# A two-layer model on one Trainium2 core: FP4 down products in three parts a block, gate and up interleaved over six PSUM banks

## The chip, the cores and the metric

The kernel runs on one core of a Trainium2 chip. The engines of that core work side by side, each from a queue of its own: TensorE (PE, with its weight loads shown apart as PEld), VectorE (DVE), ScalarE (ACT), GpSimd (POOL), and SyncE (SP), which here only issues DMAs. Matrix products land in PSUM, eight banks of 128 x 512 fp32 words, and DVE or ACT has to read a bank out before TensorE may write it again. The metric is the device time of one execution in microseconds (us).

## The reference

The input x is 2 x 1024 tokens of width 512. Four layers follow one another, each as `x = layernorm(x + layer(x))`: a linear attention, a feed-forward layer with FP4 weights, a gated linear attention in chunks of 64, and a feed-forward layer that takes the 512 best-scored tokens of a sequence. The change touches the second one alone:

```python
w_gu   = dequant_fp4(gate_up_packed, gate_up_scales)   # [2816, 512], a scale for each 128 inputs
w_down = dequant_fp4(down_packed, down_scales)         # [512, 1408]
gate_up = x @ w_gu.T
gate, up = gate_up[..., :1408], gate_up[..., 1408:]
h = silu(gate) * up
y = h @ w_down.T
y = y / sqrt(mean(y*y, axis=-1) + 1e-6)
x = layernorm(x + y)
```

All arithmetic is fp32. The gate and up products take x in two fp32r parts (x1Th, the rounded value, and x1Tl, the rest), so that two quick matmuls stand for one fp32 matmul.

## The kernel before

**Tiling.** The tokens are cut into NB = 4 blocks of 512. In the FP4 layer a block has NI = 11 passes, f = 0 to 10, one for each 128 of the 1408 hidden units. A pass makes a gate tile and an up tile, 128 units x 512 tokens each. Each is a sum over KC = 4 groups of 128 inputs, and because every group has a scale of its own the groups can't be summed in PSUM: each group (two matmuls, the x1Th one and the x1Tl one, L458) gets a bank, and the bank is then added with its scale to a tile in SBUF. Group k = 0 is written by ACT (L463, called g0 and u0 below); groups 1 to 3 are added by DVE (L468, g1 to g3 and u1 to u3). Where a pass is called `alone` or `by_three`, u3 goes to ACT (L465) and POOL (L466) instead. ACT then applies silu to the gate tile (L634), and POOL multiplies the two into a chunk of h (L635). The gate and up tiles have two rooms each, taken in turn by f.

**The down product.** y of a block is computed from h and wdn one block later, in seven-product form (Strassen's): P1 to P7 and a small P8 for the odd eleventh chunk. The function `down` is a generator that yields before each of its 78 steps; a step is one fp32 matmul of 256 columns (L501 or L510), which the trace shows as two entries. `take(pieces, n)` runs it on by n yields. POOL makes the sums that the products need (`sums`, L516), and DVE adds the products to y (L525 to L544).

**Staging.** Before the change the steps of the last block's products are spread over the passes: five yields ahead of pass 0, then eight or nine behind each of the passes 0 to 8, and none behind passes 9 and 10. During passes 9 and 10 the x of the next block is turned: eight PE transposes (L190) behind each of the two passes, then ACT copies (L204) and DVE differences (L205) that make x1Th and x1Tl. The block before that, whose y is complete, is normed in `old_steps`: ACT squares (L577), POOL takes the inverse root (`power`, L581 and L582), ACT scales y (L586), POOL adds y to x (L591), DVE takes statistics (L181, L182), POOL norms x (L560). After the four blocks a tail of seven `take` calls runs the last block's products, together with the transposes and logits of the next layer.

**Order.** A planner (Tile's scheduler) sets the order in each engine's queue. Code that comes earlier has the right of way among what it believes ready; `tc.issue_after(ins)` puts what is traced in it behind `ins` on that engine. So `issue_after(mm)` holds the order on PE, `issue_after(sl)` that on ACT behind the silu, `issue_after(hm)` that on POOL behind the product h. Engines take their queues in order.

**Banks.** Two pools of four banks: `mm_bank` serves gate, up and the transposes, `acc_bank` the products P1 to P8. In `alone` passes the groups with odd k use the second pool too, so that eight banks take turns.

Of the kernel before, what the change touches and what calls it, by code (L numbers as in the profile page):

```python
# [10 lines left out]
F32 = mybir.dt.float32  # L11
# [10 lines left out]
P = 128  # L22
B, T, C = 2, 1024, 512
NB = 4
# [49 lines left out]
def body(ctx: ExitStack, tc: tile.TileContext, a: dict, out: bass.AP):  # L74
# [7 lines left out]
    pmm = ctx.enter_context(tc.tile_pool(name="pmm", bufs=4, space=PSUM))  # L82
    pacc = ctx.enter_context(tc.tile_pool(name="pacc", bufs=4, space=PSUM))
    dram = ctx.enter_context(tc.tile_pool(name="dram", bufs=1, space=DRAM))

    def mm_bank(name):
        return pmm.tile([P, 512], F32, tag="mm", name=name)

    def acc_bank(name):
        return pacc.tile([P, 512], F32, tag="acc", name=name)  # L90
# [343 lines left out]
    with tc.tile_pool(name="s2", bufs=1) as wk2:  # L434
# [17 lines left out]
        def scaled_sum(f, parts, name, by_three, eight_banks):  # L452

            acc = rooms[name][f % 2]
            for k in range(KC):
                ps = (acc_bank if eight_banks and k % 2 else mm_bank)(f"{name}p")
                for x in parts:
                    ins = nc.tensor.matmul(  # L458
                        ps, wgu[:, k, f * P : (f + 1) * P], x[:, k], start=x is parts[0], stop=x is parts[1]
                    ).ins  # L460
                s = scale[:, k * FG + f : k * FG + f + 1]
                if k == 0:
                    nc.scalar.activation(acc, ps, AF.Copy, scale=s)  # L463
                elif k == KC - 1 and by_three:
                    nc.scalar.activation(spare, ps, AF.Copy, scale=s)  # L465
                    nc.gpsimd.tensor_add(acc, acc, spare)  # L466
                else:
                    last = nc.vector.scalar_tensor_tensor(acc, ps, s, acc, ALU.mult, ALU.add).ins  # L468
            return acc, ins, last
# [18 lines left out]
        of_S = lambda j: S[:, j]  # L488

        def down(h, y_of):  # L490

            A11, A12, A21, A22 = (h.block(e, s) for s in range(2) for e in range(2))

            def whole(name, x, w, tail=None):

                ps = acc_bank(name)
                for r in range(2):
                    cut = ps[:, 256 * r : 256 * r + 256]
                    for j in range(NP):
                        yield  # L500
                        nc.tensor.matmul(  # L501
                            cut, x(j)[:, r], w[:, j], start=j == 0, stop=j == NP - 1 and tail is None
                        )
                    if tail is not None:
                        yield
                        of_last(cut, r, *tail, start=False)
                return ps.rearrange("p (r c) -> p r c", r=2)

            def of_last(cut, r, s, o, start):
                nc.tensor.matmul(  # L510
                    cut, h.last(s)[:, r], wdn[:, NI - 1, 256 * o : 256 * o + 256], start=start, stop=True
                )

            def sums(op, dst, x, y):
                for j in range(NP):
                    ins = nc.gpsimd.tensor_tensor(dst(j), x(j), y(j), op).ins  # L516
                return ins

            sums(ALU.add, of_S, A21, A22)
            p1 = yield from whole("P1", A11, B11)  # L520
            p2 = yield from whole("P2", A12, B21, (0, 0))
            p5 = yield from whole("P5", of_S, T1)
            c11, c12, c21, c22 = y_of()
            nc.scalar.copy(c21, p1)
# [12 lines left out]
            nc.vector.tensor_add(c22, c12, p7)  # L537
            p8 = acc_bank("P8")
            for r in range(2):
                yield  # L540
                of_last(p8[:, 256 * r : 256 * r + 256], r, 1, 1, start=True)
# [20 lines left out]
        class Normed:  # L562
# [57 lines left out]

        wsums = sums_of_wdn()
        now, pieces = None, iter(())
        for blk in range(NB):
            h = Hidden(blk)
            for f in range(NI):
                if f == 0:
                    if blk:
                        with tc.issue_after(mm), tc.issue_after(hm):
                            take(pieces, 5)

                alone = blk == 0 or f >= NI - 2
                gate, mm, st = scaled_sum(f, parts, "gate", False, alone)
                up, mm, st = scaled_sum(NI + f, parts, "up", alone, alone)
                sl = nc.scalar.activation(gate, gate, AF.Silu).ins  # L634
# [762 lines left out]
```

## Time and profile before

| what | value |
|---|---|
| median of 3 runs | 1033.77 us (1033.0 to 1033.81) |
| the profiled execution's own time | 1033.33 us |
| its span, first to last instruction | 1031.6 us |
| TensorE busy in the span | 999.9 us (97%) |
| mean granted TensorE clock | 0.995 |
| stretch of the FP4 layer's four blocks | 254.3 to 554.3 us |
| its tail, to the next layer | to about 604 us |

The page gives the busy time of each engine and groups of like instructions; the timeline gives single instructions with their start, length and, in brackets, the idle time of the engine ahead of them with the instruction that ended it. A matmul of 512 columns is shown some 0.40 us long, but such matmuls overlap: what one costs is the distance from its start to the next start. All of what follows is read in that way.

### The profile page before, as it was taken

To read this page: it belongs to the slowest core of one execution; us is meant where nothing else is said; L and a number is where in the kernel's file an instruction comes from. 1 tells how busy PE (TensorE), PEld (TensorE's weight loads), DVE (VectorE), ACT (ScalarE), POOL (GpSimd) and SP (SyncE) were. 2 spreads that over 40 slices of the span, in tenths; PEclk is the share of its full clock that TensorE was granted. 3 is DMA by queue.
4 is the path that set the end of the run, shared out by engine and by line. 5 is a ranking of instruction groups with operands and counts; after the bars stand their busy time and mean duration, and the time that the engine had idled before them with its cause. 6 is when DMAs were issued, how large, how long until landed. Compare 5 with 4: busy or idle time off the path is not lost.

```text
span 1031.6 us, 10932 instructions
## 1 busy us (share of the span) xinstructions
PE 999.9 (97%) x4061; PEld 706.7 (69%) x4061; DVE 651.5 (63%) x1225; ACT 283.9 (28%) x469; POOL 306.1 (30%) x281
## 2 busy tenths in 40 slices
PE   8999999999999998999999999999999999999996
PEld 3454444545767776777778955687687688888885
DVE  1246745376875675675677139446788886689744
ACT  2223232222652244234324043242121123221000
POOL 1100351003785634554556403101005003000022
PEclk9999999999999999999999999999999999999999
DMA  9611123100000000000002050000002422140011
GB/s 346 194 46 56 42 69 98 31 31 0 1 1 1 1 1 0 1 1 1 1 0 93 1 213 1 1 1 1 1 1 82 124 81 82 41 141 24 1 41 41
DMA packets 25688, 48.81 MB, mean 47 GB/s; under 512 B 4652, under 2 KB 6316, under 8 KB 25123
## 3 DMA queue, kind: packets, MB, share of 16 engines
q1 hardware_dynamic: 22995, 42.85, 12.5%
q0 software_dynamic: 1920, 4.22, 1.1%
q10 hardware_dynamic: 720, 1.05, 0.3%
q8 instruction: 32, 0.52, 0.2%
q14 instruction: 21, 0.17, 0.1%
HBM read 39.70 MB, written 10.52 MB: 49 GB/s over the span
## 4 chain that ended last, share of the span: by engine, by line
PE 71%; DVE 10%; issue 9%; ACT 5%; POOL 4%; DMA 0%; POOLq 0%; DVEq 0%; ACTq 0%
PE P L501 11%; PE yp L1141 9%; PE hp L1062 7%; PE qp L210 5%; PE xk L279 5%; PE upp L458 5%; PE ao L210 5%; PE kp L210 4%; DVE gate L468 3%; PE gatep L458 3%; PE ao L945 3%; PE go L901 2%; ACT gate L463 2%; PE kp L296 1%; PE lp L425 1%
## 5 line engine op out<-in xcount | busy, mean ns | idle before, releaser
L468 DVE SCALAR_TENSOR_TENSOR gate<-gatep,scale,gate 128x512 f32<-128x512 f32 x132 | 98.6, 749 | 76.2 <-ACT gate L463 69.8
L174 POOL TENSOR_TENSOR rs<-rs,table 128x4 f32<-128x4 f32 (+1 forms) x21 | 19.6, 936 | 321.2 <-DVE rs L173 320.7
L468 DVE SCALAR_TENSOR_TENSOR up<-upp,scale,up 128x512 f32<-128x512 f32 x115 | 85.9, 747 | 8.1 <-ACT up L463 1.5
L458 PE MATMUL upp<-x1Th,wgu 128*128 128x512 f32 x176 | 75.8, 432 | 10.6 <-ACT gate L463 7.9
L458 PE MATMUL gatep<-x1Th,wgu 128*128 128x512 f32 x176 | 74.5, 430 | 1.2 <-ACT x1Th L204 1.1
L458 PE MATMUL upp<-x1Tl,wgu 128*128 128x512 f32 x176 | 70.5, 403 | 0.0
L458 PE MATMUL gatep<-x1Tl,wgu 128*128 128x512 f32 x176 | 68.6, 399 | 0.1
L635 POOL TENSOR_TENSOR h<-up,gate 128x512 f32<-128x512 f32 x32 | 40.8, 1276 | 87.8 <-DVE up L468 79.7
L501 PE MATMUL P<-wdn,h 128*128 128x256 f32 x256 | 61.9, 379 | 0.0
L458 PEld LDWEIGHTS upp<-x1Th,wgu 128*128 128x128 f32 x176 | 33.6, 191 | 38.2 <-DVE gate L468 18.2
L463 ACT ACTIVATE gate<-gatep,scale 128x512 f32<-128x512 f32 x44 | 30.3, 688 | 104.3 <-PE gatep L458 89.7
L210 PE MATMUL ao<-G,qT 128*128 128x512 f32 x128 | 57.6, 595 | 0.0
L210 PE MATMUL qp<-Wq,x0T 128*128 128x512 f32 x128 | 57.6, 592 | 0.0
L279 PE MATMUL xk<-k,x 128*128 128x512 f32 x128 | 56.7, 592 | 0.0
L945 PE MATMUL ao<-W1o,uT 128*128 128x512 f32 x128 | 55.6, 592 | 0.0
L501 PEld LDWEIGHTS P<-wdn,h 128*128 128x128 f32 x256 | 48.2, 190 | 6.7
L849 POOL TENSOR_TENSOR sum<-sum,sq 128x512 f32<-128x512 f32 x12 | 19.0, 1582 | 107.8 <-issue 84.5
L264 DVE SCALAR_TENSOR_TENSOR k<-kp,e 128x512 f32<-128x512 f32 x16 | 11.0, 691 | 55.4 <-ACT e L263 49.4
L279 PEld LDWEIGHTS xk<-k,x 128*128 128x128 f32 x128 | 24.3, 190 | 30.6 <-issue 29.9
L210 PEld LDWEIGHTS ao<-G,qT 128*128 128x128 f32 x128 | 24.0, 190 | 30.0 <-issue 28.7
L945 PEld LDWEIGHTS ao<-W1o,uT 128*128 128x128 f32 x128 | 24.0, 190 | 28.7 <-issue 28.0
L210 PE MATMUL kp<-Wk,x0T 128*128 128x512 f32 x96 | 43.3, 593 | 0.2 <-DVE k L264 0.2
(335 smaller groups left out, 2131.0 us busy)
## 6 DMA issues: line engine op xcount, KB each, us to landing
pk<-in_gu SPq DMA_DIRECT2D x16, 352.0 KB, 3.8
x<-in_x SPq DMA_DIRECT2D x4, 1024.0 KB, 12.8
w<-in_w SPq DMA_DIRECT2D x1, 4096.0 KB, 14.5
xs<-picked SPq DMA_DIRECT2D x4, 1024.0 KB, 5.0
out<-x SPq DMA_DIRECT2D x4, 1024.0 KB, 4.3
w<-in_w SPq DMA_DIRECT2D x4, 1024.0 KB, 6.4
x0T<-in_xT SPq DMA_DIRECT2D x3, 1024.0 KB, 8.8
pk<-in_dn SPq DMA_DIRECT2D x11, 256.0 KB, 3.5
```

What stands on the lines that cost most here:

```text
L174: power = nc.gpsimd.tensor_tensor(rs[:, :n], rs[:, :n], const("mhalf")[:, :n], ALU.pow).ins
L210: nc.tensor.matmul(ps, lhs[:, k], w[:, k], start=start and k == 0, stop=stop and k == KC - 1)
L279: nc.tensor.matmul(acc[c], x_t[2 * b + i // 4][:, i % 4, c * P : (c + 1) * P], k, start=i == 0, stop=i == 7)
L458: ins = nc.tensor.matmul(ps, wgu[:, k, f * P : (f + 1) * P], x[:, k], start=x is parts[0], stop=x is parts[1]).ins
L463: nc.scalar.activation(acc, ps, AF.Copy, scale=s)
L468: last = nc.vector.scalar_tensor_tensor(acc, ps, s, acc, ALU.mult, ALU.add).ins
L501: nc.tensor.matmul(cut, x(j)[:, r], w[:, j], start=j == 0, stop=j == NP - 1 and tail is None)
L635: hm = nc.gpsimd.tensor_mul(h.chunk(f), up, gate).ins
L901: nc.tensor.matmul(ps[:, 256 * m : 256 * m + 256], w[:, k, m], b[:, k, 256 * half : 256 * half + 256], start=k == 0, stop=k == KC - 1,)
L945: nc.tensor.matmul(ao[i], uT[blk][:, k, i * P : (i + 1) * P], W1o[:, k], start=n == 0, stop=n == 3)
L1062: nc.tensor.matmul(ps[:, 256 * j : 256 * j + 256], w[:, k, 2 * g + j], x[:, k], start=k == 0, stop=k == 1)
L1141: nc.tensor.matmul(ps[:, 256 * r : 256 * r + 256], x(r, j), w(j), start=j == 0, stop=j == NJ - 1)
```

## The change

It does five things, all in the FP4 layer.

1. The steps of the down product are no longer spread. Pass 0 starts the generator with one yield (the POOL sums alone, no matmul); 22 steps (P1, P2) run behind pass 2, 32 (P5, P4, P6) behind pass 5 and 24 (P7, P8, P3) behind pass 8.
2. Each product is added to y as soon as it ends, where before the adding of P1 and P2 waited for the end of P5, and that of P4 and P5 for the end of P6. For that, y's room is asked for after P1, not after P5.
3. Gate and up take turns group by group (`scaled_sums`): g0, u0, g1, u1, and so on, each pass behind the last matmul of what went before. Gate, up and transposes get six banks (0 to 3, 6, 7), the products two (4, 5); `alone` is gone, and u3 goes to ACT and POOL in block 0 and in passes 9 and 10, as before. In the tail the banks are four and four again.
4. The rooms of the gate and up tiles alternate over the whole layer, so that pass 0 no longer takes the room that pass 10 has just used.
5. Of the old block's norm, the inverse root moves from step 1 to step 0, statistics and the first two tiles' norm to step 2. In block 3 the squares and the root of block 2 are traced behind pass 9, and the rest of that norm ahead of the tail.

```diff
-    pmm = ctx.enter_context(tc.tile_pool(name="pmm", bufs=4, space=PSUM))
-    pacc = ctx.enter_context(tc.tile_pool(name="pacc", bufs=4, space=PSUM))
+    psum = ctx.enter_context(tc.tile_pool(name="psum", bufs=1, space=PSUM))
+    rings, turn_of = {"mm": range(4), "acc": range(4, 8)}, {"mm": 0, "acc": 0}
+    def bank(ring, name):
+        i = rings[ring][turn_of[ring] % len(rings[ring])]
+        turn_of[ring] += 1
+        return psum.tile([P, 512], F32, tag=f"bank{i}", name=name)
...
-        def scaled_sum(f, parts, name, by_three, eight_banks):
-
-            acc = rooms[name][f % 2]
+        def scaled_sums(f, parts, gate, up, by_three):
+
             for k in range(KC):
...
+                for acc, at, name in ((gate, f, "gatep"), (up, NI + f, "upp")):
+                    ps = mm_bank(name)
+                    for x in parts:
+                        ins = nc.tensor.matmul(
+                            ps, wgu[:, k, at * P : (at + 1) * P], x[:, k], start=x is parts[0], stop=x is parts[1]
+                        ).ins
+                    s = scale[:, k * FG + at : k * FG + at + 1]
+                    if k == 0:
+                        nc.scalar.activation(acc, ps, AF.Copy, scale=s)
+                    elif k == KC - 1 and acc is up and by_three:
+                        nc.scalar.activation(spare, ps, AF.Copy, scale=s)
+                        nc.gpsimd.tensor_add(acc, acc, spare)
+                    else:
+                        last = nc.vector.scalar_tensor_tensor(acc, ps, s, acc, ALU.mult, ALU.add).ins
+            return ins, last
...
             p1 = yield from whole("P1", A11, B11)
-            p2 = yield from whole("P2", A12, B21, (0, 0))
-            p5 = yield from whole("P5", of_S, T1)
             c11, c12, c21, c22 = y_of()
             nc.scalar.copy(c21, p1)
+            p2 = yield from whole("P2", A12, B21, (0, 0))
             nc.vector.tensor_add(c11, c21, p2)
+            p5 = yield from whole("P5", of_S, T1)
+            nc.vector.tensor_add(c12, c21, p5)
             ins = sums(ALU.subtract, of_S, of_S, A11)
+            with tc.issue_after(ins):
+                ins = sums(ALU.subtract, A21, A11, A21)
+            with tc.issue_after(ins):
+                sums(ALU.subtract, A12, A12, of_S)
             p4 = yield from whole("P4", A22, T4, (1, 0))
-            with tc.issue_after(ins):
-                sums(ALU.subtract, A21, A11, A21)
+            nc.vector.tensor_add(c21, c21, p4)
             p6 = yield from whole("P6", of_S, T2)
-            nc.vector.tensor_add(c12, c21, p6)
-            nc.vector.tensor_add(c21, c12, p4)
-            nc.vector.tensor_add(c12, c12, p5)
-            sums(ALU.subtract, A12, A12, of_S)
+            nc.vector.tensor_add(c12, c12, p6)
+            nc.vector.tensor_add(c21, c21, p6)
             p7 = yield from whole("P7", A21, B12)
+            nc.vector.tensor_add(c22, c12, p7)
             nc.vector.tensor_add(c21, c21, p7)
-            nc.vector.tensor_add(c22, c12, p7)
             p8 = acc_bank("P8")
...
                 return {
-                    0: lambda: self.squares(range(4)),
-                    1: lambda: (self.power(), self.scaled(), self.to_x((0, 1))),
-                    2: lambda: self.to_x((2, 3)),
-                    4: self.stats,
-                    5: lambda: self.norm((0,)),
-                    7: lambda: self.norm((1,)),
+                    0: lambda: (self.squares(range(4)), self.power()),
+                    1: lambda: (self.scaled(), self.to_x((0, 1))),
+                    2: lambda: (self.to_x((2, 3)), self.stats(), self.norm((0, 1))),
                     8: lambda: self.norm((2, 3)),
                 }
...
+        rings["mm"], rings["acc"] = (0, 1, 2, 3, 6, 7), (4, 5)
...
-                if f == 0:
-                    if blk:
-                        with tc.issue_after(mm), tc.issue_after(hm):
-                            take(pieces, 5)
-
-                alone = blk == 0 or f >= NI - 2
-                gate, mm, st = scaled_sum(f, parts, "gate", False, alone)
-                up, mm, st = scaled_sum(NI + f, parts, "up", alone, alone)
+                if f == 0 and blk:
+                    with tc.issue_after(hm):
+                        take(pieces, 1)
+                gate, up = (rooms[n][(blk * NI + f) % 2] for n in ("gate", "up"))
+                with tc.issue_after(mm) if blk or f else ExitStack():
+                    mm, st = scaled_sums(f, parts, gate, up, blk == 0 or f >= NI - 2)
                 sl = nc.scalar.activation(gate, gate, AF.Silu).ins
                 hm = nc.gpsimd.tensor_mul(h.chunk(f), up, gate).ins
                 with tc.issue_after(mm), tc.issue_after(st), tc.issue_after(hm), tc.issue_after(sl):
-                    if f < NI - 2:
-                        take(pieces, 9 if f in (0, NI - 3) else 8)
                     if blk == 0 and f in (2, 4, 6, 8):
                         norm_tiles(3, late, (f // 2 - 1,))
-                    for _ in range((2, 2, 2, 0, 1, 1)[f] if blk == 1 and f < 6 else 0):
+                    for _ in range((1, 1, 4, 1, 1)[f] if blk == 1 and f < 5 else 0):
                         next(wsums)
                     if blk > 1 and f in old_steps:
                         old_steps[f]()
+
+                    if blk and f in (2, 5, 8):
+                        take(pieces, {2: 22, 5: 32, 8: 24}[f])
+                        mm = last_p[0]
...
+                        if blk == NB - 1 and f == NI - 2:
+                            now.squares(range(4))
+                            now.power()
...
+        rings["mm"], rings["acc"] = range(4), range(4, 8)
+        with tc.issue_after(st):
+            for _ in old.rest():
+                pass
         for n, steps in enumerate((11, 12, 10, 12, 10, 10, 14)):
             with tc.issue_after(mm), tc.issue_after(hm):
                 take(pieces, steps)
-            if n == 0:
-                old.squares(range(4))
-                old.power()
-            if n == 1:
-                for _ in old.rest():
-                    pass
```

More of the change, by code (lines that the diff above doesn't have):

```diff
@@ L81, in body @@
     sp = ctx.enter_context(tc.tile_pool(name="small", bufs=3))
-    pmm = ctx.enter_context(tc.tile_pool(name="pmm", bufs=4, space=PSUM))
-    pacc = ctx.enter_context(tc.tile_pool(name="pacc", bufs=4, space=PSUM))
+    psum = ctx.enter_context(tc.tile_pool(name="psum", bufs=1, space=PSUM))
     dram = ctx.enter_context(tc.tile_pool(name="dram", bufs=1, space=DRAM))
+    rings, turn_of = {"mm": range(4), "acc": range(4, 8)}, {"mm": 0, "acc": 0}
[3 more added lines that the diff above has]
+        return psum.tile([P, 512], F32, tag=f"bank{i}", name=name)
     def mm_bank(name):
-        return pmm.tile([P, 512], F32, tag="mm", name=name)
+        return bank("mm", name)
     def acc_bank(name):
-        return pacc.tile([P, 512], F32, tag="acc", name=name)
+        return bank("acc", name)
     table = cpool.tile([P, _TABLE.shape[1]], F32, name="table")
@@ L450, in sums_of_wdn @@
                     yield nc.gpsimd.tensor_sub(dst[:, j], x[:, j], y[:, j])
-        def scaled_sum(f, parts, name, by_three, eight_banks):
-            acc = rooms[name][f % 2]
+        def scaled_sums(f, parts, gate, up, by_three):
             for k in range(KC):
[L456 to L469, printed above, removed]
+                for acc, at, name in ((gate, f, "gatep"), (up, NI + f, "upp")):
[13 more added lines that the diff above has]
+            return ins, last
         class Hidden:
@@ L488, in body @@
         of_S = lambda j: S[:, j]
+        last_p = [None]
         def down(h, y_of):
@@ L500, in whole @@
                         yield
-                        nc.tensor.matmul(
+                        last_p[0] = nc.tensor.matmul(
                             cut, x(j)[:, r], w[:, j], start=j == 0, stop=j == NP - 1 and tail is None
-                        )
+                        ).ins
                     if tail is not None:
                         yield
-                        of_last(cut, r, *tail, start=False)
+                        last_p[0] = of_last(cut, r, *tail, start=False)
                 return ps.rearrange("p (r c) -> p r c", r=2)
             def of_last(cut, r, s, o, start):
-                nc.tensor.matmul(
+                return nc.tensor.matmul(
                     cut, h.last(s)[:, r], wdn[:, NI - 1, 256 * o : 256 * o + 256], start=start, stop=True
-                )
+                ).ins
             def sums(op, dst, x, y):
@@ L540, in down @@
                 yield
-                of_last(p8[:, 256 * r : 256 * r + 256], r, 1, 1, start=True)
+                last_p[0] = of_last(p8[:, 256 * r : 256 * r + 256], r, 1, 1, start=True)
             nc.vector.tensor_add(c22, c22, p8.rearrange("p (r c) -> p r c", r=2))
```

## The prediction, made before the changed kernel was run

> **What bounds the kernel now.** I read the page first, then the four blocks as stretches, then one pass on PE, DVE and ACT.
>
> Page, parts 1 and 2:
>
> ```profile
> span 1031.6 us, 10932 instructions
> ...
> PE 999.9 (97%) x4061; PEld 706.7 (69%) x4061; DVE 651.5 (63%) x1225; ACT 283.9 (28%) x469; POOL 306.1 (30%) x281
> ...
> PE   8999999999999998999999999999999999999996
> ```
>
> PE is the bound nearly everywhere, so the change can win only where PE waits between 254 and 604 us. How much that is must come from starts, not from busy time. Blocks 1, 2 and 3 in the view of stretches (length, then busy time of PE, PEld, DVE, ACT, POOL, granted clock):
>
> ```profile
> 301.70:384.40 82.70, 80.26 (x349) 62.67 (x349) 54.56 (x77) 25.76 (x40) 43.53 (x42) 1.00 0.00 0
> 384.40:470.70 86.30, 81.73 (x348) 63.62 (x348) 56.86 (x86) 30.98 (x52) 45.80 (x45) 0.98 0.00 1
> 470.70:554.30 83.60, 79.90 (x340) 62.19 (x341) 54.39 (x82) 31.47 (x57) 45.88 (x46) 0.98 0.04 13
> ```
>
> The same matmuls back to back, by their spacing in the PE timeline: a gate or up matmul 0.234 us, so a pass of 16 takes 3.74; a down step 2 x 0.216 = 0.432; eight transposes 0.87. A whole block is 11 x 3.74 + 78 x 0.432 + 2 x 0.87 = 76.6 us (74.9 in block 3's stretch, which has four steps less). So 6.1, 9.7 and 8.7 us are waits. One ordinary pass, on PE:
>
> ```profile
> 357.05 0.58 PE L458 MATMUL gatep<-x1Th,wgu 128*128 128x512 f32 x1
> ...
> 359.84 0.40 PE L458 MATMUL upp<-x1Tl,wgu 128*128 128x512 f32 x1
> 360.36 0.50 PE L458 MATMUL upp<-x1Th,wgu 128*128 128x512 f32 x1
> ...
> 364.66 0.59 PE L458 MATMUL gatep<-x1Th,wgu 128*128 128x512 f32 x1
> ```
>
> From pass to pass 7.61 us, against 3.74 + 8 x 0.432 = 7.20. The loss sits at 359.84 to 360.36: u2 needs a bank that DVE hasn't read. DVE itself:
>
> ```profile
> 358.70 2.46 DVE L468 SCALAR_TENSOR_TENSOR gate<-gatep,scale,gate 128x512 f32<-128x512 f32 x3 [0.75 <-ACT gate L463]
> 361.08 2.45 DVE L468 SCALAR_TENSOR_TENSOR up<-upp,scale,up 128x512 f32<-128x512 f32 x3
> ...
> 408.22 0.74 DVE L468 SCALAR_TENSOR_TENSOR gate<-gatep,scale,gate 128x512 f32<-128x512 f32 x1
> 408.88 1.60 DVE L468 SCALAR_TENSOR_TENSOR up<-upp,scale,up 128x512 f32<-128x512 f32 x2
> ```
>
> Three additions to one tile take 2.46, 0.82 each; where a gate follows on an up (408.22 to 408.88) the distance is 0.66. Next, the large wait of block 2, pass 2 (block 3 has its twin at 491.9), from the timelines of ACT and PE and the stretch behind:
>
> ```profile
> 402.36 2.56 ACT L586 ACTIVATE y<-y,ms 128x512 f32<-128x512 f32 x4 [4.53 <-POOL ms L582]
> 404.82 0.67 ACT L463 ACTIVATE gate<-gatep,scale 128x512 f32<-128x512 f32 x1
> 405.54 0.50 PE L458 MATMUL upp<-x1Th,wgu 128*128 128x512 f32 x1 [2.67 <-ACT gate L463]
> 406.00:410.00 4.00, 3.94 (x11) 2.77 (x10) 3.37 (x6) 1.32 (x2) 0.00 (x0) 0.57 0.00 0
> ```
>
> The scaling of y stands ahead of g0 in ACT's queue and waits for POOL's root; PE idles 2.67 us and then runs at a granted clock of 0.57. Last, the border between blocks (PE, then ACT):
>
> ```profile
> 381.06 1.03 PE L190 MATMUL x1Tp<-table,x 128*128 128x128 f32 x8
> 381.93 1.89 PE L501 MATMUL P<-wdn,h 128*128 128x256 f32 x8
> 384.37 0.97 PE L458 MATMUL gatep<-x1Th,wgu 128*128 128x512 f32 x3 [0.55 <-ACT x1Th L204]
> ...
> 382.73 0.63 ACT L634 ACTIVATE gate<-gate 128x512 f32<-128x512 f32 x1 [0.72 <-DVE gate L468]
> 383.27 1.05 ACT L204 CAST x1Th<-x1Tp 128x512 fp32r<-128x512 f32 x2
> ```
>
> The next block can't start before the casts, which stand behind the silu of pass 10; four down steps (1.73 us) fill that hole today.
>
> **The waits, summed.** From starts of passes: (A) passes 1 to 8 without the two large waits lose 9.2 us (22 passes, 0.34 to 0.75 each). (B) The two passes 2, 12.02 and 11.76 us long instead of 7.20, lose 9.4. (C) Passes 0 last 9.69, 8.75 and 8.78 instead of 7.63, 4.3. (D) The borders, start of pass 9 to next pass 0: 11.66 and 11.65 against 10.97; with the first one like them, 2.1. (E) Block 0 waits about 2.1 (ACT's g0 waits for POOL's h). Together 27.1 us: the most that can be won.
>
> **Interleaving and six banks.** DVE's six additions cost 6 x 0.66 = 3.96 a pass in place of 4.9, ACT's g0 and u0 run beside. Passes 0 to 2, 3 to 5 and 6 to 8 now follow without products between. In such a run DVE starts 1.86 us behind PE and falls back 0.22 a pass. Six banks let PE lead by 6 x 0.47 = 2.8 us; followed bank by bank, the first to be late is u2 of the third pass, by 0.1. Nine runs, 0.9 us. The products then give DVE 9.5, 13.8 or 10.4 us to catch up, so (A) is gone but for that. In block 0 POOL has 7.24 us per two passes (four at 1.29, one norm tile at 2.08) against PE's 7.49; I leave 0.4 of (E).
>
> **Two banks for products.** P3 takes P7's bank while P8 (0.86 us) is all that lies between. Two additions at 0.66 and the 0.28 from matmul to DVE make some 1.65, so PE waits 0.8. Three blocks, 2.4. The others have four us or more between end and reuse: nothing; if DVE were late there, each would cost up to 0.7. y's room comes free only when POOL has added y to x behind pass 2; P1's copy then waits, but its bank is next used by P5, behind pass 5: nothing. POOL's sums for P6 (5 x 0.71 = 3.6 us from the end of P5) end 1.4 us before P6.
>
> **Norm steps.** The four squares take 3.0 us of ACT (0.75 each), the scaling 2.56, and no product lies there any more to cover them. ACT's own work is 3 x 0.58 = 1.7 a pass, so in three passes (11.2 us) there is room; what counts is the order. g0 of the next pass is there 0.92 us after that pass starts, u0 at 1.39, the silu only when DVE has ended g3, about 1.6: g0 and u0 should precede the silu and all behind it. Then g0 of pass 2 comes about 1 us late, inside the banks' lead: 0.5 in blocks 2 and 3, 1.0 in place of (B). The root behind POOL's h of pass 0 waits for the squares, and h of pass 1 behind it by about 1 us; nobody needs that room before pass 3. In block 3 the squares traced behind pass 9 have the right of way over u0 of pass 10: at worst that comes 3.3 us late, at best 0.7; I take 2.0. SP's queue has nothing moved past it. The tail keeps its order (DVE did the old norm at 555.2 anyway): 0, plus or minus 0.5.
>
> **The border.** This is what speaks against. Of five yields four were matmuls, and now none is left. Passes 9 and 10 also drop from eight banks to six: the turned quarters hold banks through cast and difference, and g2 of pass 10 waits about 0.9. Then g3 of pass 10, now DVE's last addition, ends 1.9 us after the matmuls, silu 0.63, casts 1.05. Followed through, pass 0 starts 12.8 after pass 9; if DVE never idled it would be 11.5. I take 12.5, against work of 9.24: 3.3 a border, 9.8 for three. Rooms that alternate let g0 go sooner, so of (C) I keep 0.3 each, 0.9.
>
> **Two rules against rows.** PE would then idle 2 to 2.7 us at each border. Both idles of 2.67 in this trace were followed by a slow spell: 0.57 in the stretch above, and 0.60 from 492 to 496 us, about 1.7 us each. The Trainium skill, "TensorE: Matmul & The Clock Gate", part 1, says that the clock halves after at least one idle window of about 3.4 us, a window that runs freely. By the rule a border costs no clock (sum 1023.6 us), by the row 1.7 each (1028.7). Idles of 1.1 us show no spell, so I take half: 2.6. And "Perfetto Trace Analysis", Matmul Optimizations, wants all eight banks in use. Passes 9 and 10 with eight banks show 8.35 us, no wait; by the rule the 0.9 there and P3's 0.8 are the price of splitting, 5.1 us in all (with eight 1021.1). I keep my counts, since six banks cover the longer stretch.
>
> **The sum.** New waits 0.9 + 2.4 + 1.0 + 0.9 + 9.8 + 2.6 + 0.4 + 2.0 = 20.0, old ones 27.1: 7.1 us less than the profiled execution's 1033.3, **1026.2 us**. That execution lies 0.4 under the median of 1033.8; a difference of 0.2%, 2.1 us, is about what a measurement can tell.
>
> **Rivals.** (1) *ACT's queue, slower.* If the planner puts squares and scaling ahead of u0 or g0, u0 of pass 1 is free 9.6 us after pass 0 starts instead of 7.0, a wait of 2.6; the scaling adds 2.2 in pass 2, with one spell of 1.7: 6.5 a block, 13 in two in place of 1.0, and 3.3 in place of 2.0 in block 3: 1039.5. For it: L586 did just this at 402.36, and traced code has the right of way. Against: in block 0 g0 went ahead of an older silu (266.74 before 267.32). It ends slower once the five places lose over 1.4 us each beyond my count. (2) *Kind borders.* Passes 0 at 11.3 and no slow spell: 3.6 and 2.6 us better, 1020. For it: before, the casts came 2.2 after the matmuls of pass 10. (3) *The interleaving doesn't reach DVE*: gate first, then up, at 0.82: DVE falls back 1.2 a pass, 2.5 us a run, nine runs: 1048. Against: PE's order is fixed group by group.
>
> **Chances.** Forecast 0.56, (2) 0.17, (1) in full or in half 0.22, (3) 0.02, the rest 0.03. The forecast's own spread is some 4 us, half of (1) lies around 1033. That makes faster 0.71, same 0.11, slower 0.18. The range 1018 to 1037 takes in (2) with its borders at the floor and half of (1).
>
> **What would show it.** Right: 3.74 to 3.9 us from pass to pass in the runs; DVE's L468 at 0.66; no u2 wait; 1 us or less in passes 1 and 2 of blocks 2 and 3; 12 to 13 us from pass 9 to pass 0 with a cast as releaser; a clock under 1 behind some borders; P3 0.8 late. Wrong: ACT's L577 or L586 ahead of g0 or u0 with PE idle over 2 us, borders under 11 or over 14, or a pass over 4.2.

## The result, and the profile after

The changed kernel takes **1024.81 us** (median of 4 runs, 1024.43 to 1025.64), the kernel before, on the same chip, 1033.79 (4 runs, 1033.0 to 1035.17): 0.9913 of the time, 95% interval 0.9896 to 0.993. The forecast was 1026.2 with a range of 1018 to 1037. The profiled execution took 1025.06 us (1033.33 before).

The page of the changed kernel, parts 1 and 2:

```profile
span 1023.2 us, 10989 instructions
...
PE 992.5 (97%) x4061; PEld 708.1 (69%) x4061; DVE 643.9 (63%) x1229; ACT 278.2 (27%) x469; POOL 303.8 (30%) x281
...
PE   8999999999989999998999999999999999999996
PEclk9999999999999999999999999999999999999999
```

PE's share is the same 97%: its busy time fell by 7.4 us with the same 4061 instructions, so part of the waiting, and matmuls at a lower clock, count as busy. In the row of tenths the 8 at 387 to 413 us, the large wait of block 2, is gone, and two others stand at 281 to 307 and 460 to 486 us: borders between blocks. As before, only starts tell what was lost. The blocks 1, 2 and 3 as stretches (length, busy time of PE, PEld, DVE, ACT, POOL, granted clock), then the first 3.4 us of blocks 1 and 2 by themselves:

```profile
302.46:386.09 83.63, 79.56 (x349) 65.03 (x349) 51.46 (x78) 23.99 (x40) 42.49 (x42) 0.98 0.00 0
386.09:467.81 81.72, 78.00 (x348) 63.81 (x349) 54.37 (x87) 29.20 (x52) 45.79 (x45) 1.00 0.00 1
467.81:546.50 78.69, 77.62 (x344) 63.25 (x345) 51.76 (x83) 28.28 (x53) 43.72 (x43) 1.00 0.04 14
303.00:306.40 3.40, 3.40 (x9) 2.63 (x9) 0.65 (x2) 1.27 (x2) 3.33 (x5) 0.51 0.00 0
386.20:389.60 3.40, 3.40 (x15) 2.77 (x16) 1.70 (x4) 1.27 (x2) 3.40 (x6) 1.00 0.02 5
```

Block 2, which lost most before, went from 86.30 to 81.72. Block 1 starts at half the clock (9 matmuls where block 2 has 15). A run of passes on PE, from the start of pass 4 of block 2 to the start of pass 5, and to the first product behind it:

```profile
411.05 0.40 PE L465 MATMUL gatep<-x1Th,wgu 128*128 128x512 f32 x1
...
414.79 0.39 PE L465 MATMUL gatep<-x1Th,wgu 128*128 128x512 f32 x1
...
418.69 0.38 PE L509 MATMUL P<-T,S 128*128 128x256 f32 x1
```

3.74 us for a pass: PE waits for no bank in it. DVE beside it takes gate and up in turn, 0.66 from start to start:

```profile
413.61 0.74 DVE L475 SCALAR_TENSOR_TENSOR up<-upp,scale,up 128x512 f32<-128x512 f32 x1
414.26 0.74 DVE L475 SCALAR_TENSOR_TENSOR gate<-gatep,scale,gate 128x512 f32<-128x512 f32 x1
414.92 0.74 DVE L475 SCALAR_TENSOR_TENSOR up<-upp,scale,up 128x512 f32<-128x512 f32 x1
```

ACT in block 2, where before g0 of pass 2 stood behind the scaling of y:

```profile
394.02 0.63 ACT L587 ACTIVATE rw<-y 128x512 f32<-128x512 f32 x1
394.56 0.19 ACT L587 ACTIVATION_READ_ACCUMULATOR rw<-y 128x1 f32 x1
394.65 0.67 ACT L470 ACTIVATE gate<-gatep,scale 128x512 f32<-128x512 f32 x1
395.23 0.62 ACT L587 ACTIVATE rw<-y 128x512 f32<-128x512 f32 x1
...
395.84 0.68 ACT L470 ACTIVATE up<-upp,scale 128x512 f32<-128x512 f32 x1
396.41 0.62 ACT L640 ACTIVATE gate<-gate 128x512 f32<-128x512 f32 x1
397.37 2.56 ACT L596 ACTIVATE y<-y,ms 128x512 f32<-128x512 f32 x4 [0.34 <-POOL ms L592]
```

g0 slips in ahead of the fourth square, and the scaling (397.37) comes behind u0 and the silu. The new waits, each with its releaser in brackets: P3 for P7's bank (DVE, PE), and the border (PE, then ACT):

```profile
449.00 0.68 DVE L547 TENSOR_TENSOR y<-y,P 128x512 f32<-128x512 f32 x1
449.83 1.97 PE L509 MATMUL P<-wdn,h 128*128 128x256 f32 x8 [0.60 <-DVE y L547]
...
463.05 0.47 PE L465 MATMUL gatep<-x1Th,wgu 128*128 128x512 f32 x1 [0.86 <-DVE x1Tl L212]
464.52 1.04 PE L197 MATMUL x1Tp<-table,x 128*128 128x128 f32 x8
467.81 0.50 PE L465 MATMUL gatep<-x1Th,wgu 128*128 128x512 f32 x1 [2.25 <-ACT x1Th L211]
...
466.17 0.63 ACT L640 ACTIVATE gate<-gate 128x512 f32<-128x512 f32 x1 [0.69 <-DVE gate L475]
466.70 1.05 ACT L211 CAST x1Th<-x1Tp 128x512 fp32r<-128x512 f32 x2
```

Pass 10 waits for the bank of a turned quarter, and pass 0 for the casts that stand behind the silu of pass 10: PE is idle for 2.25 us at 467.81, where four product steps lay before.

**Where the time went.** The FP4 layer, from its first pass to the next layer, went from 342.5 us to 336.1 in the profiled executions: 6.4 less. The other 1.8 lie outside it (0.9 ahead, about 0.9 behind), where the code is the same. In the kernels below the second pass of block 0 starts anywhere from 257.0 to 258.2 us with the same code ahead of it, so this part is not ascribed to the change.

### The profile page after: what moved, and what is told of

It is laid out like the page before. It is cut to its first block, busy times and chain, and to the rows that moved or that the text cites. A ratio compares the mean times of both kernels' runs of the same rounds, so it can differ in the third digit from the quotient of the medians.

```text
span 1023.2 us, 10989 instructions
## 1 busy us (share of the span) xinstructions
PE 992.5 (97%) x4061; PEld 708.1 (69%) x4061; DVE 643.9 (63%) x1229; ACT 278.2 (27%) x469; POOL 303.8 (30%) x281
## 4 chain that ended last, share of the span: by engine, by line
PE 82%; issue 8%; DVE 5%; ACT 3%; POOL 2%; DMA 0%; POOLq 0%; DVEq 0%; ACTq 0%
PE P L509 12%; PE yp L1150 9%; PE hp L1071 9%; PE gatep L465 8%; PE upp L465 8%; PE qp L217 5%; PE xk L286 5%; PE ao L217 5%; PE kp L217 4%; PE ao L954 3%; PE go L910 2%; PE kp L303 1%; PE lp L432 1%; PE P L518 1%; PE up L827 1%
## 5 line engine op out<-in xcount | busy, mean ns | idle before, releaser
L465 PE MATMUL upp<-x1Th,wgu 128*128 128x512 f32 x176 | 70.4, 404 | 0.5 <-ACT up L470 0.5
L465 PEld LDWEIGHTS gatep<-x1Th,wgu 128*128 128x128 f32 x176 | 33.1, 189 | 26.3 <-ACT x1Th L211 7.5
L188 DVE BATCH_NORM_STATS2 st<-x 128x6 f32<-128x512 f32 x64 | 43.1, 685 | 5.1 <-POOL x L601 4.3
```

The source lines that it names most:

```text
L188: nc.vector.bn_stats(st, x)
L465: ins = nc.tensor.matmul(ps, wgu[:, k, at * P : (at + 1) * P], x[:, k], start=x is parts[0], stop=x is parts[1]).ins
```

## The experiments

Each is one edit of the changed kernel (1024.8 us) unless said otherwise; times are medians, and the ratio is to the kernel before, measured beside it.

**1. Six product steps back at the border.**

```diff
-                    with tc.issue_after(hm):
-                        take(pieces, 1)
+                    with tc.issue_after(mm), tc.issue_after(hm):
+                        take(pieces, 7)
+                    mm = last_p[0]
...
-                        take(pieces, {2: 22, 5: 32, 8: 24}[f])
+                        take(pieces, {2: 16, 5: 32, 8: 24}[f])
```

> The changed kernel with six matmul steps of P1 put back ahead of passes 0 of blocks 1 to 3 (taken from the 22 behind pass 2, so that the work stays the same). Theory, the border is a hole behind the casts (2.25 us idle each in the changed kernel's trace, and one slow spell worth 1.7 us behind the first): six steps are 2.6 us and fill it, border from the start of pass 9 to pass 0 unchanged at 12.9 us with the steps inside, no idle over 0.5 us there, and 3 x 2.3 + 1.7 = 8.6 us less: 1016. Rival, PE's total wait there is set by something else (DVE or ACT, which get no more time to catch up), so that the steps only push pass 0 back: border 15.2 us, time 1024.8. A loss of more than 1 us would say that the queue of P1 (its first half waits for POOL's h of pass 10) stands ahead of pass 0.

Measured: 1016.17 us, ratio 0.9835 (0.9821 to 0.9849). PE at the border from block 2 to 3:

```profile
458.67 1.04 PE L197 MATMUL x1Tp<-table,x 128*128 128x128 f32 x8
459.55 1.89 PE L509 MATMUL P<-wdn,h 128*128 128x256 f32 x8
...
461.95 0.58 PE L465 MATMUL gatep<-x1Th,wgu 128*128 128x512 f32 x1
```

From pass 9 to pass 0 it is still 12.9 us, but 2.6 of them are now work, and no slow spell follows. The border is a hole, and six steps in it take 8.6 us off. (Before the change four lay there.)

**2. The three parts undone.**

```diff
-                    if blk and f in (2, 5, 8):
-                        take(pieces, {2: 22, 5: 32, 8: 24}[f])
+                    if blk and f < NI - 2:
+                        take(pieces, 9 if f in (0, NI - 3) else 8)
```

(with five yields ahead of pass 0, as before)

> The changed kernel with the three parts undone alone: four matmul steps ahead of passes 0 and eight or nine behind each of passes 0 to 8, as in the kernel before; interleaving, six banks, additions at a product's end and the early steps of the norm stay. Theory, the interleaving and the banks carry the gain: passes at 7.2 to 7.3 us, the 2.2 us idle of each border mostly filled by the four steps (1.7 us each, and the one slow spell gone), P3's wait of 0.77 gone because passes lie between P7 and P3: 1024.8 - 5.2 - 1.7 - 2.3 + 1 = about 1017. Rival, the three parts carry it (products between every two passes cost PE a wait each time): passes at 7.5 to 7.6 again, nine of 0.3 in three blocks, 1025 to 1033.

Measured: 1033.74 us, ratio 1.0007 (1.0 to 1.0013). The whole gain is gone, as the rival said, but not for its reason. Passes with eight steps take 7.18 to 7.20 us, which is their work, and block 1 takes 79.57 us, as in experiment 1. Nearly all that experiment 1 has over this kernel is lost in the passes 2 of blocks 2 and 3, 15.59 and 15.94 us long (POOL, ACT, PE):

```profile
403.61 2.48 POOL L601 TENSOR_TENSOR x<-x,y 128x512 f32<-128x512 f32 x2
...
406.12 0.59 ACT L530 COPY y<-P 128x512 f32<-128x512 f32 x1 [3.88 <-POOL x L601]
...
406.76 1.65 PE L509 MATMUL P<-T,S 128*128 128x256 f32 x3 [5.90 <-ACT y L530]
```

PE idles 5.90 us and then runs at half the clock to 411.29. P1's copy needs y's room, which is free only when POOL has added the old y to x; P5 needs P1's bank; with products spread from pass 0 on, P5 comes before that. Since the change asks for y's room at P1's end, P5 has to wait until pass 3, and three parts do that. (P3's wait for P7's bank is in this kernel too: passes 7, with eight steps, take 8.42.)

**3. Spread, but with P5 not before pass 3** (the line of 2 changed once more, four steps ahead of pass 0 as there).

```diff
+                    if blk and f < NI - 2:
+                        take(pieces, (6, 6, 6, 11, 11, 10, 8, 8, 8)[f])
```

> The three parts undone once more (four steps ahead of pass 0, products behind each of passes 0 to 8), but with P5 not begun before pass 3: 6, 6, 6, 11, 11, 10, 8, 8, 8 steps. Theory: spreading lost its 8.4 and 8.75 us in the passes 2 of blocks 2 and 3 (and nothing elsewhere, 7.18 us a pass) because P1's copy waits for y's room and P5 for P1's bank; three parts matter only for keeping P5 behind pass 2. Then 1033.7 - 17.2 = 1016.5, as good as three parts with the border covered. Rival: products between every two passes cost something by themselves in blocks 2 and 3, where ACT has squares and scaling as well: 1020 or more.

Measured: 1019.97 us, ratio 0.9867 (0.9852 to 0.9883): 13.8 of the 17.2 come back, so y's room is the reason. The rest is 0.85 in each of two passes (the copy is still that late) and P3's wait, 1.66 a block here, since P7's additions stand behind six of a pass. Not the 1016.5 that I expected.

**4. Gate first, then up.**

```diff
-            for k in range(KC):
-                for acc, at, name in ((gate, f, "gatep"), (up, NI + f, "upp")):
+            for acc, at, name in ((gate, f, "gatep"), (up, NI + f, "upp")):
+                for k in range(KC):
```

> The changed kernel with the interleaving undone alone: the four gate groups of a pass, then its four up groups; three parts and six banks stay. Theory, DVE's three additions to one tile follow each other at 0.82 us instead of 0.66, so DVE takes 4.9 us a pass against PE's 3.74 and falls back by 1.2 a pass: passes 1 and 2 of a run at 4.5 to 4.9 us, some 2 us lost in each of nine runs and 3 in block 0: 1044 to 1048. Rival, the order in which PE is fed does not matter because DVE may take gate and up in turn (two passes overlap): 1025 to 1030.

Measured: 1036.96 us, ratio 1.0033 (1.0022 to 1.0044): 12.1 more, between theory and rival. (Single executions differ: four of 14 took 1033.8 to 1034.8 at a granted clock of 0.995 to 0.997, the other ten 1036.7 to 1037.5 at 0.992; the profile is one of the ten.) DVE:

```profile
337.61 0.75 DVE L475 SCALAR_TENSOR_TENSOR up<-upp,scale,up 128x512 f32<-128x512 f32 x1 [0.34 <-PE upp L465]
338.27 0.74 DVE L475 SCALAR_TENSOR_TENSOR gate<-gatep,scale,gate 128x512 f32<-128x512 f32 x1
338.93 0.74 DVE L475 SCALAR_TENSOR_TENSOR up<-upp,scale,up 128x512 f32<-128x512 f32 x1
...
342.88 2.32 DVE L475 SCALAR_TENSOR_TENSOR up<-upp,scale,up 128x512 f32<-128x512 f32 x3
```

Inside a run the planner mixes the ups of a pass with the gates of the next, at 0.66; only at the end of a run do three ups follow each other, 0.79 apart ((2.32 - 0.74) / 2). So a block loses 3.0 us in its runs and not 7.5; block 0 loses 3.0, and two more borders are followed by a slow spell (1.5 each); two borders are 1.2 shorter.

**5. Four banks and four.**

```diff
-        rings["mm"], rings["acc"] = (0, 1, 2, 3, 6, 7), (4, 5)
+        rings["mm"], rings["acc"] = range(4), range(4, 8)
```

> The changed kernel with four banks for gate and up and four for products, as before; three parts and interleaving stay. Theory, four banks let PE lead DVE by 1.9 us instead of 2.8: every third pass of a run loses 0.5 us, the second 0.2 (nine runs, 6 us), P3 no longer waits for P7's bank (minus 2.3), the turned quarters of pass 9 and 10 hold half of the banks (plus 3 over three borders): 1030 to 1033. Rival, DVE keeps up with PE at 0.66 and the two banks were not needed: 1022 to 1025.

Measured: 1055.14 us, ratio 1.021 (1.0193 to 1.0226), far beyond both. Block 0 takes 3.9 us more, block 1 5.3, block 2 8.6, block 3 12.1; second passes of a run take 5.4 to 5.9 us in place of 3.73 to 3.91. And the old wait of block 2 is back (ACT, PE):

```profile
406.69 2.56 ACT L596 ACTIVATE y<-y,ms 128x512 f32<-128x512 f32 x4 [0.72 <-POOL ms L592]
409.15 0.67 ACT L470 ACTIVATE gate<-gatep,scale 128x512 f32<-128x512 f32 x1
...
409.87 0.50 PE L465 MATMUL gatep<-x1Th,wgu 128*128 128x512 f32 x1 [2.27 <-ACT gate L470]
```

The scaling stands ahead of g0 again, and PE waits 2.27 us for g0's bank. So the planner's order on ACT has changed with the number of banks, and not only PE's lead.

**6. Five banks and three** (`(0, 1, 2, 3, 6), (4, 5, 7)`).

> The changed kernel with five banks for gate and up and three for products. With four and four it took 1055.1, 30 us more, against 5 to 8 that the lead alone (0.47 us a bank) gave. Theory, the loss is a threshold: with four banks the second pass of a run finds g0 late on ACT (its bank is needed 1.9 us after g0's matmuls, and ACT gives it back 2 us after them), and the two scalings of y ahead of g0 cost 2.4 us and a slow spell each; five banks cover most of that: 1026 to 1030, with P3's wait of 0.77 gone. Rival, each bank is worth the same: half of the 30 us, 1040.

Measured: 1031.66 us, ratio 0.9984 (0.9978 to 0.999): 6.8 more than with six, where the theory gave up to 5.2. The fifth bank is worth 23.5 us, the sixth 6.8: not a price a bank. On ACT g0 stands ahead of the scaling here (399.13 and 400.79 in block 2), as with six, so the threshold of the theory and the queue's order come together. P3's wait is gone (from the start of pass 8 to pass 9 it is 14.53 us, not 14.91).

**7. Spread as in 3, with four banks and four** (1019.97 us with six and two).

> Products behind every pass again (6, 6, 6, 11, 11, 10, 8, 8, 8 steps, four ahead of pass 0; 1020.0 us with six and two banks), with four banks for gate and up and four for products. Theory, six banks are needed only because three passes follow each other: with products between, DVE needs 3.96 us in 6.3 to 8.5 and four banks do; P3's wait for P7's bank (1.6 us a block in that arrangement) goes, so 1016 to 1020. Rival, four banks cost PE a wait in every pass, as they did before the change (0.34 to 0.75): 1028 or more.

Measured: 1029.86 us, ratio 0.9973 (0.9961 to 0.9984); neither was right. Block 1 takes 79.04 us, and its passes have no wait (7.18 to 7.20 with eight steps): with products between, four banks and interleaving do, and the rival falls. But block 0, which has no products, loses 3.9 us as in experiment 5, and in blocks 2 and 3 something late on ACT reaches PE at once (ACT, PE):

```profile
409.71 0.59 ACT L530 COPY y<-P 128x512 f32<-128x512 f32 x1 [1.92 <-POOL x L601]
410.19 0.69 ACT L470 ACTIVATE up<-upp,scale 128x512 f32<-128x512 f32 x1
...
410.94 0.50 PE L465 MATMUL upp<-x1Th,wgu 128*128 128x512 f32 x1 [2.07 <-ACT up L470]
```

P1's copy, waiting for y's room, stands ahead of u0. In experiment 3, with six banks, the same copy is as late, but u0 stands ahead of it:

```profile
402.86 0.68 ACT L470 ACTIVATE up<-upp,scale 128x512 f32<-128x512 f32 x1
405.50 0.58 ACT L530 COPY y<-P 128x512 f32<-128x512 f32 x1 [1.97 <-POOL x L601]
```

**8. The norm's steps as before.**

```diff
-                    0: lambda: (self.squares(range(4)), self.power()),
-                    1: lambda: (self.scaled(), self.to_x((0, 1))),
-                    2: lambda: (self.to_x((2, 3)), self.stats(), self.norm((0, 1))),
+                    0: lambda: self.squares(range(4)),
+                    1: lambda: (self.power(), self.scaled(), self.to_x((0, 1))),
+                    2: lambda: self.to_x((2, 3)),
+                    4: self.stats,
+                    5: lambda: self.norm((0,)),
+                    7: lambda: self.norm((1,)),
```

> The changed kernel (1024.8 us) with the steps of the old block's norm alone put back: squares behind pass 0, root and scaling behind pass 1, statistics behind pass 4, norm tiles behind 5, 7 and 8. Theory: it was ACT's scaling, waiting for POOL's root at the head of its queue, that cost the passes 2 of blocks 2 and 3 their 2.67 us and the slow spell behind; with the root traced behind pass 0 it is early enough. So both waits come back: 2 x (2.7 + 1.7) = 8.8, 1033.6. Rival: with interleaving, six banks and alternating rooms g0 goes ahead anyway, wherever the root stands: 1025 to 1026.

Measured: 1029.73 us, ratio 0.9965 (0.9951 to 0.9979): 4.9 more, and neither number. On the scaling the rival is right: its wait does not come back, g0 goes ahead (394.38, the scaling at 399.53), and passes 0 to 2 of block 2 take 3.84, 3.90 and 13.30, as in the changed kernel. What comes is something else (POOL, PE):

```profile
426.38 2.07 POOL L570 TENSOR_SCALAR x<-x,mv,rs 128x512 f32<-128x512 f32 x1
428.43 2.08 POOL L524 TENSOR_TENSOR S<-S,h 128x256 f32<-128x256 f32 x3
...
429.20 4.91 PE L509 MATMUL P<-T,S 128*128 128x256 f32 x18 [0.69 <-POOL S L524]
```

A norm tile gets between POOL's sums for P6, and P6 follows them at POOL's pace: 1.7 us in blocks 2 and 3. One more border has a slow spell (1.5).

**9. Rooms by f's parity** (`[f % 2]` in place of `[(blk * NI + f) % 2]`).

> The changed kernel with the alternation of rooms alone undone: a room by f's parity, so that pass 0 of a block takes the room of pass 10 of the block before. The prediction put 3.4 of the 4.3 us that passes 0 lost before down to this (its term C): then g0 of pass 0 waits for POOL's h of pass 10 (1.29 us behind the silu) and pass 0 loses about 1.1 us in each of three blocks: 1028.2. Rival: at the new borders h of pass 10 has long ended when g0 of pass 0 comes (pass 0 starts 2.2 us after its matmuls could), so the alternation carries nothing: 1024.8, and C went with the order of the queue and the six banks instead.

Measured: 1025.13 us, ratio 0.9918 (0.9903 to 0.9934): the rival holds, passes 0 of blocks 2 and 3 take the same 3.84 us, and that of block 1 5.39 with its slow spell, as in the changed kernel. (With steps ahead of pass 0 it wasn't tried.)

**10. The norm tiles of x's last block moved from block 0 to block 1,** on top of experiment 1 (1016.17 us).

```diff
-                    if blk == 0 and f in (2, 4, 6, 8):
-                        norm_tiles(3, late, (f // 2 - 1,))
+                    if blk == 1 and f in (3, 4, 6, 7):
+                        norm_tiles(3, late, ((3, 4, 6, 7).index(f),))
```

> The kernel with six steps ahead of passes 0 (1016.2 us), and with the four norm tiles of x's last block moved from block 0 (behind passes 2, 4, 6, 8) to block 1 (behind passes 3, 4, 6, 7). Theory for block 0: two of its passes take 7.96 us because POOL's round is four operations of 1.29, one norm tile of 2.08 and an idle 0.7 that it waits for ACT's silu; without the norm tile the round is below PE's 7.47 and passes 2 to 9 take 3.74 to 3.8: 1.6 to 1.8 us less, 1014.5. Rival, ACT's order (b behind POOL, g0 behind b) sets the round, not POOL's work: unchanged at 1016.2, or worse if the tiles push h back in block 1, where POOL also forms the sums of the down weights.

Measured: 1013.51 us, ratio 0.9806 (0.9793 to 0.982). In the changed kernel ACT and POOL held each other up (POOL, then ACT):

```profile
270.51 2.08 POOL L570 TENSOR_SCALAR x<-x,mv,rs 128x512 f32<-128x512 f32 x1
272.56 1.29 POOL L473 TENSOR_TENSOR up<-up,b 128x512 f32<-128x512 f32 x1
...
273.88 0.69 ACT L472 ACTIVATE b<-upp,scale 128x512 f32<-128x512 f32 x1 [2.10 <-POOL up L473]
```

b waits for POOL's addition, that for the norm tile, and g0 stands behind b. Without the tile the passes 4 to 8 take 3.73 to 3.74 us, not 3.91 to 4.19. It took off 2.7 where I expected 1.6 to 1.8: the border behind block 0 got shorter too, 12.65 us instead of 13.31.

**11. P3 behind pass 9,** on top of experiment 1.

```diff
-                    if blk and f in (2, 5, 8):
-                        take(pieces, {2: 16, 5: 32, 8: 24}[f])
+                    if blk and f in (2, 5, 8, 9):
+                        take(pieces, {2: 16, 5: 32, 8: 12, 9: 12}[f])
```

> The kernel with six steps ahead of passes 0 (1016.2 us), and with P3's twelve steps moved from behind pass 8 to behind pass 9. Theory: P3's wait of 0.77 for P7's bank goes, since a pass of 3.74 lies between, and the wait of 1.0 in pass 10 for the bank of a turned quarter goes too, since DVE has P3's 5.2 us to catch up before the quarters are turned: 1.8 us in each of three blocks, 1011. Rival, the wait in pass 10 stays, since it is the casts and differences themselves that last: 0.8 a block only, 1014. Against both: the next block's casts write the tile that P3 reads, so they must follow it; if that delays them the border grows and the gain is lost, 1016 or more.

Measured: 1009.87 us, ratio 0.977 (0.9757 to 0.9783), 6.3 less. Both waits are gone: from the start of pass 8 to pass 9 it is 8.89 us (work 3.74 + 12 x 0.432 = 8.92), and from pass 9 to pass 0, with P3 and six steps of P1 in it, 17.0 (work 9.22 + 18 x 0.432 = 17.0).

**12. Experiments 1, 10 and 11 together.**

> The three edits that each took something off, together: six steps of P1 ahead of passes 0, P3 behind pass 9, the norm tiles of x's last block in block 1. Theory, they remove different waits and add up: 1024.8 - 8.6 - 6.3 - 2.7 = 1007.2. Rival, they share a wait (POOL's h or the border): over 1008.5.

Measured: **1007.57 us** (5 runs, 1007.08 to 1008.36), ratio 0.9754 (0.9738 to 0.9769). They add up. The blocks 1 and 2 of this kernel as stretches:

```profile
299.92:377.56 77.64, 77.27 (x351) 64.03 (x349) 51.61 (x80) 24.20 (x40) 51.83 (x47) 1.00 0.00 1
377.56:454.67 77.11, 77.11 (x351) 64.12 (x349) 54.19 (x87) 29.10 (x52) 45.71 (x45) 1.00 0.00 1
```

Against 76.6 of work a block; PE shows no idle time in block 2.

## Why the prediction was right, and where not

The new waits, from the starts of the passes in the profile after, against the terms of the sum:

| term | forecast | measured |
|---|---|---|
| runs, norm steps and passes 0 (0.9 + 1.0 + 0.9) | 2.8 | 2.4 |
| P3 for P7's bank | 2.4 | 2.4 (0.8 each) |
| borders (13.31, 12.90, 12.91 less 9.24 each) | 9.8 | 11.4 |
| slow spells | 2.6 | 1.5 (one) |
| block 0, passes 1 to 8 | 0.4 | 1.8 |
| block 3, pass 10 (4.81 less 3.74) | 2.0 | 1.1 |
| sum | 20.0 | 20.6 |

The sum held because its errors cancel, which is luck. Against 27.1 of old waits it leaves 6.5, and the layer became 6.4 shorter.

**Interleaving: right, for half of its size.** DVE at 0.66 and passes at 3.74 came as said, and without it the kernel is slower than before (experiment 4). Rival 3 had the right mechanism but put 22 us on it; 12.1 were measured, because neighbouring passes mix on DVE. (The 0.82 of the prediction is the length of three additions divided by three. From start to start it is (2.46 - 0.74) / 2 = 0.86 before and 0.79 in experiment 4.)

**Old waits (A).** It is not the banks that remove them: block 1 of experiment 7 has four, and no wait in passes 1 to 8. Interleaving is the likely reason, but no run takes it out with products behind every pass. The adding of each product at its end, POOL's earlier sums and PE's fixed order of passes were in all these kernels; their own shares stay open.

**The two large waits (B): gone, and the reason given was half of it.** The prediction rested on g0 and u0 going ahead on ACT, which the trace shows. Experiment 8 shows that the root's earlier place has no part in that. With four banks the wait is back (experiment 5), so the banks are needed. How they act is only in part shown: in both kernels with four the planner put the late instruction ahead of the one that frees PE's bank (the scaling ahead of g0, P1's copy ahead of u0), and with more banks behind it. Whether six banks would cover a late ACT in the same order was not tried. Banks were priced by DVE's backlog alone, in the prediction and still in what was expected of experiment 5 (some 6 us in the runs); the two that gate and up gained are worth 30 here, order and slow spells taken in. What rival 1 feared (squares and scaling ahead of PE's next bank) showed itself only with four.

**Passes 0 (C): wrong cause.** The prediction credited the alternating rooms with 3.4 us. Experiment 9 puts that at nothing: pass 0 now starts 2.25 us late anyhow. Which of the other parts took the old wait away was not separated.

**The border: the mechanism right, the size 0.4 a border short.** 12.9 against 12.5, where following it through had given 12.8; the first, behind block 0, takes 13.3. Casts as the releaser and the wait of 0.9 in pass 10 came as named. Rival 2, kind borders, did not.

The other price of splitting the banks (put at 5.1 us in the prediction, beside the rule of all eight banks in the Trainium skill, "Perfetto Trace Analysis", Matmul Optimizations) was real, 0.8 and 1.0 us a block; but experiment 11 took both waits away with six and two, by order alone.

**Mis-sized.** Block 0 (0.4, measured 1.8): the working counted POOL's work, 7.24 us of 7.49, as if POOL could always run; but POOL waits 0.7 for ACT's silu, ACT for POOL, and a round takes 7.96. Experiment 10 shows it. Block 3's pass 10 (2.0, measured 1.1): one square stood ahead of u0, not all.

**The clock: near by luck.** The two ends of that term were none and three spells; there was one of three. Neither the rule of the Trainium skill ("TensorE: Matmul & The Clock Gate", part 1), read as a whole idle window of 3.4 us, nor the row of before, where both idles had one, held for all three. The half was taken for want of knowledge, and the last section shows what decided: how each idle lay on a grid of windows, which the prediction named but did not weigh.

## What to carry to other kernels

Work taken out from between two stages may have been the cover of a hole at their border: look for what PE waits on once it is gone, and leave as many steps there as the hole is long (here six at each of three borders took off 8.6 us). Banks are not only a lead over the engine that reads them most: with their number the order of a second reader's queue changed too, and their worth was uneven (30 us for two, 23.5 of it for the first). So look at that queue's order beside the banks. And when parts of a change depend on one another (here an early request for a room, and when the products that need it run), undoing one alone measures the dependence; it takes a second version that keeps it to see what the part is worth.

## What the runs showed of the hardware

The clock halved after shorter idles than 2.67 us, and not each time. In the changed kernel and in experiments 6, 8 and 9 PE idled 2.0 to 2.3 us at twelve borders; five were followed by matmuls at 0.427 us in place of 0.234, a loss of 1.5 us. In experiment 4 all three borders were, though PE's two idles there, with transposes between them, were of 0.7 to 1.5 and 1.0 us. In experiments 1, 10, 11 and 12, with the border covered, none was.

The traces show what tells the twelve apart. From the second pass of block 0 to the last block's end a stretch of granted clock 0.50 lasts 3.41 us (or 6.83, after the 5.9 us of experiment 2), and where a trace has several they begin whole multiples of 3.413 us apart: in experiment 4 at 306.34, 391.67 and 477.01, which is 25 of them each time. So there is a grid of windows, and PE's idle time in the one window ahead counts. The grid does not lie alike in every trace: with the same work ahead, the slow stretch begins 0.2, 0.4 and 1.2 us behind the start of block 1 in experiment 8, the changed kernel and experiment 9. In experiment 9 (length, busy time of PE; the granted clock is the third number from the end), first a border with a slow spell and then one without, each with the window that follows:

```profile
300.96:304.37 3.41, 1.17 (x5) 0.98 (x6) 1.86 (x3) 1.59 (x3) 3.28 (x4) 1.00 0.00 0
304.37:307.78 3.41, 3.41 (x10) 2.64 (x9) 1.63 (x3) 1.26 (x2) 2.71 (x4) 0.50 0.00 0
382.88:386.29 3.41, 1.64 (x12) 1.22 (x10) 2.24 (x5) 1.85 (x4) 1.63 (x2) 1.00 0.00 0
386.29:389.70 3.41, 2.93 (x13) 2.38 (x14) 1.70 (x3) 1.59 (x3) 3.41 (x5) 1.00 0.02 5
```

Both idles are 2.25 us long. The first lies whole in one window, the second is cut by the grid, and 1.77 is the most that one window gets. So it is with all twelve: 2.25 to 2.28 us idle in one window ahead of the five slow spells, at most 1.18 to 1.77 at the other seven. Over all traces of this case, in the same part of the kernel, 2.0 us or more of idle in a window at full clock was always followed by the half clock and 1.55 or less never; in between both occur (1.62, 1.63 and 1.87 slow, in experiments 4 and 5; 1.64, 1.72 and 1.77 not), and what decides there stays open. That fits the freely running window of 3.4 us that the Trainium skill ("TensorE: Matmul & The Clock Gate", part 1) tells of, but not that a whole window must be idle.
